# Perceiver block on one core: the row maxima go along the partitions by two DMAs through DRAM, and the second value product stands later in its slot

## The chip, the cores and the metric

The kernel runs on one core of a Trainium2 chip. The metric is device time in microseconds (us); smaller is better. The engines are named as in the profile: PE is TensorE's matrix product, PEld its weight load, DVE is VectorE, ACT ScalarE, POOL GpSimd and SP SyncE, which here only issues DMAs.

## The reference

A block of three parts on x (32 batches x 64 queries x 256), all in float32:

```python
# cross attention: 16 heads of 16 features, 1601 keys in each batch
qh = split_heads(layernorm(x) @ wq.T + bq)
kh = split_heads(ctx @ wk.T + bk)            # ctx: 32 x 1601 x 256
vh = split_heads(ctx @ wv.T + bv)
scores = where(mask, einsum('bhqd,bhkd->bhqk', qh, kh) / sqrt(16), -1e9)
x = x + merge(softmax(scores) @ vh) @ wo.T + bo

# span attention over the 64 queries: no keys, a weight by distance
span = heads(layernorm(x) @ W_span.T)        # two numbers for each query and head
mean, soft = sigmoid(span[..., 0]) * 64, softplus(span[..., 1])
x = x + merge(softmax(-soft * (pos - mean) ** 2) @ heads(h @ W_val.T)) @ W_out.T

# a shared gated unit and 2 of 8 experts, chosen by the token's number
x = x + ffn(layernorm(x))
```

What matters for the change is the softmax of the cross attention: from each score, the largest score of its query and head is taken off before the exponential.

## The kernel before, in words

**Tiles.** The work of the cross attention comes in 64 halves n = 0 to 63: batch b = n // 2 and, with c = n % 2, 8 of its 16 heads. The keys are padded to 13 chunks of 124. Scores stand with the keys along the partitions: `prob` keeps them as 124 partitions x (pair of heads j) x 13 chunks x 128, where 128 is two heads by 64 queries. A pair is 124 x 1664 numbers. A half has four pairs, j = 0 to 3. `prob` has five places of two pairs: pairs 0 and 1 of half n are in place n % 2, pairs 2 and 3 in place 2 + n % 3.

**Steps of a half.** TensorE projects keys (`pk`, L492, in four groups of 4, 3, 3 and 3 chunks, numbered 0 to 3) and values (`pv`, L492, in units of two chunks, numbered 0 to 6). ACT copies them out of PSUM into kT (L507) and v (L524). `scores(n, g)` with g = 0, 1, 2 computes 4, 5 and 4 chunks of scores (`psc`, L546), and DVE adds the mask while it moves them into `prob` (L570). The fifth chunk of g = 1 does not fit in the four PSUM banks of the others. It goes to one bank more and to `spare_pvs`, and DVE moves it with two adds of its own, which stand as A and B in the lists of order (L563). `spare_pvs` lies in the same PSUM tile as `pvs`, where the value products are summed. ACT copies the first chunk into `mrun` (L579), and DVE takes the running maximum over the 13 chunks (L587); the last one writes `mx`.

**The maxima.** `mx` still has 124 partial maxima, one in each partition. TensorE transposes it (`pm`, L594) and DVE reduces it along the row to `mc` (L601), 128 x 4: the maximum of each column of `prob`, with the column along the partitions. It is needed in every partition. So `maxima_along_rows` has TensorE transpose each column of `mc`, repeated 124 times, into a bank `pb` (L609), and ACT copies that to `mb` (L613), 128 x 4 x 128, one buffer. `less_maxima` (L618) takes it off a pair on POOL, in the last half on DVE. `exponentials` (L623) run on ACT, and `values` (L633) multiply the exponentials by the values into `pvs`; `values(n, r)` takes pairs 2r and 2r + 1.

**The order.** Inside `tc.manual_schedule` (L729) each of PE, DVE, ACT and POOL carries out its instructions in the order in which the program names them; SP is not in that list and is ordered by the scheduler. The loop at L766 has 63 slots, n = 0 to 62. Slot n finishes half n - 1, works on the maxima and the exponentials of half n, and computes the scores of half n + 1 and the projections of batch b + 1. A slot reads:

```python
values(n-1, 0); project_keys(0); steps(-1); exponentials(n-1, 3)
scores(n+1, 0, taken_off)         # with the transposes into pm, and mc between its adds
project_values(3) if c else project_keys(1)
m = maxima_along_rows(mc); less_maxima(n, 0)
run(3*n); values(n-1, 1)
scores(n+1, 1); exponentials(n, 0)
# c = 1: keys 1, values 4, keys 2     c = 0: keys 2, values 0, values 1
less_maxima(n, 1); steps(1); exponentials(n, 1); less_maxima(n, 2)
scores(n+1, 2); project_keys(3)
# c = 1: values 5, 6                  c = 0: values 2
less_maxima(n, 3); exponentials(n, 2)
```

Some projections are `tiled`: `product` (L483) then splits one into four that use 32 columns of TensorE's array each. `run` and `steps` carry on the generators `query_steps` (L449, the first layer norm and the queries of two batches) and `span_steps` (L239, the span attention of two batches). Its 23 steps are spread over STEPS (L232), in stretches of a third of a slot, so it comes round once in four slots. Two of its steps are spoken of later: POOL's product with the reciprocal total (L349) and PE's transposes of its result, `psa` (L357), one stretch later. The other PE steps are `po`, `po2`, `po3`, `pval`, `psp`, and `tr_q`, `pq`, `tr_h` and `tr_f` for queries and norms. POOL also carries out three small steps for each layer norm (L206 to L209).

**PSUM and loads.** All banks named here but `mrun` and `pvs` come from one pool of six, in turn; whoever takes a bank waits until its last reader is done. `piece_ahead` has SP load a piece of the context two batches ahead (`ct`, five buffers of 3 or 4 chunks each, 361 to 496 KB), `load_x` loads two batches of x (128 KB, five buffers). The feed-forward part follows at L905.

Of the kernel before, what the change touches and what calls it, by code (L numbers as in the profile page):

```python
# [15 lines left out]
F32 = mybir.dt.float32  # L16
U8 = mybir.dt.uint8
AF = mybir.ActivationFunctionType
ALU = mybir.AluOpType
AX = mybir.AxisListType  # L20
PSUM = bass.MemoryType.PSUM
IN_TURN = mybir.DependencyInfo(mybir.DependencyClass.Sync, mybir.DependencyReason.DATA)

P = 128
S = 64
D = 256
# [4 lines left out]
CHUNK = 124  # L31
NKC = 13
# [58 lines left out]
def perceiver_kernel(ctx: ExitStack, tc: tile.TileContext, a: dict[str, bass.AP], out: bass.AP):  # L91
    nc = tc.nc
# [7 lines left out]
    work = ctx.enter_context(tc.tile_pool(name="work", bufs=2))  # L100
# [21 lines left out]
    xs: dict[int, bass.AP] = {}  # L122
    kept = ctx.enter_context(tc.tile_pool(name="kept", bufs=1, space=bass.MemoryType.DRAM))
    x_kept = kept.tile([NTILE, P, D], F32, name="x_kept")

    def load_x(t: int):
        xs[t] = work.tile([P, D], F32, tag="x", bufs=5, name=f"x{t}")
        nc.sync.dma_start(out=xs[t], in_=a["x"][t * P : (t + 1) * P, :])

    def load_square(name: str, engine, width: int = D):  # L130
# [352 lines left out]
    def piece_ahead(b: int, g: int):  # L483
        if b < B:
            load_piece(b, g)
# [116 lines left out]
            col, ps[:, : 4 * CHUNK].rearrange("p (j k) -> p j k", j=4), AX.X, ALU.max  # L602
        )

    def maxima_along_rows(col):

        ps = mm_bank("pb")
        for j in range(4):
            nc.tensor.transpose(  # L609
                ps[:CHUNK, j * P : (j + 1) * P], col[:, j : j + 1].to_broadcast([P, CHUNK]), ident  # L610
            )
        m = work.tile([P, 4, P], F32, tag="mb", bufs=1, name="mb")
        nc.scalar.copy(m[:CHUNK].rearrange("p j q -> p (j q)"), ps[:CHUNK])  # L613
        return m

    def less_maxima(n: int, j: int, m, engine):
        sj = pair_of(n, j)
        engine.tensor_tensor(  # L618
            sj, sj, m[:CHUNK, j, None, :].to_broadcast([CHUNK, NKC, P]), ALU.subtract
        )  # L620

    def exponentials(n: int, j: int):
        nc.scalar.activation(pair_of(n, j), pair_of(n, j), AF.Exp)  # L623

    def values(n: int, r: int):

        b, c = halves[n]
        v = vs[b % 2]
        for k in range(NKC):
            kn = min(CHUNK, KEYS - k * CHUNK)  # L630
            for j in range(4):
                h = 4 * r + j
                nc.tensor.matmul(  # L633
                    pvs[32 * j : 32 * j + DK + 1, c, :, r, :],
                    lhsT=v[:kn, k, 8 * c + h, :],
                    rhs=pair_of(n, h // 2)[:kn, k, (h % 2) * S : (h % 2) * S + S],
                    start=(k == 0), stop=(k == NKC - 1), tile_position=(0, 32 * j),
                )
# [64 lines left out]
    def finish_steps(b: int, stretch: int):  # L703

        t = b // 2
        if b % 2 == 0:
            oT[t] = work.tile([P, 2, 2, S], F32, tag="oT", name=f"oT_{t}")
        flat = "p c u r q -> p (c u r q)"
        nc.vector.transpose(turned_pvs.rearrange(flat), pvs.rearrange(flat))
        by_head = turned_pvs.rearrange("p c u r i -> p (c u r) i")  # L710
        rec = work.tile([P, 8], F32, tag="rec", name=f"rec_{b}")
        nc.vector.reciprocal(rec, by_head[:, :, DK])
        o = work.tile([P, 8, DK], F32, tag="o", name=f"o_{b}")
        nc.vector.tensor_tensor(
            o, by_head[:, :, :DK], rec[:, :, None].to_broadcast([P, 8, DK]), ALU.mult
        )
        nc.vector.transpose(oT[t][:, :, b % 2, :], o.rearrange("p (c n) i -> p c (n i)", c=2))
        if b % 2:
            at = steps_of(t)
            agenda[stretch - 1 + at[0]].append((t, span_steps(t, oT.pop(t))))  # L720
            held_at.add(stretch - 1 + at[SMALL])
        yield
# [7 lines left out]
        tc.manual_schedule(  # L730
            engines={
                mybir.EngineType.PE, mybir.EngineType.DVE, mybir.EngineType.Activation,
                mybir.EngineType.Pool,
            }
        )
    )
# [25 lines left out]
        load_piece(1, g)  # L762
    last = len(halves) - 1

    extra = {3 * last - 3: (0,), 3 * last - 2: (1, 2, 4), 3 * last - 1: (5, 6)}
    for n, (b, c) in enumerate(halves[:-1]):  # L766
        if c == 0:
            piece_ahead(b + 2, 0)
            if b % 2 == 0 and b // 2 + 1 < NTILE:
                load_x(b // 2 + 1)  # L770
        if c and b % 2 == 0 and b // 2 + 1 < NTILE:
            agenda[3 * n].append((b // 2 + 1, query_steps(b // 2 + 1)))

        def project(f, *args):
            if b + 1 < B:
                f(b + 1, *args)

        def steps(g: int):
            run(3 * n + g)
            for u in extra.get(3 * n + g, ()):  # L780
                linear_factor(u)

        def taken_off():
            turned.extend(turned_maxima(n))
            return turned

        turned: list = []
        if n:
            values(n - 1, 0)
        project(project_keys, c, 0, True)  # L790
        if n:
            steps(-1)
            exponentials(n - 1, 3)
        if c:
            piece_ahead(b + 2, 1)
        scores(n + 1, 0, taken_off)
        if c:
            project(project_values, 3)
        else:
            project(project_keys, c, 1)  # L800
        m = maxima_along_rows(turned[1])
        less_maxima(n, 0, m, nc.gpsimd)
        held = 3 * n in held_at
        if not held:
            first_maxima(n + 1)
        run(3 * n)
        if n:
            values(n - 1, 1)
            if c == 0:
                agenda[3 * n + 1].append((b // 2, finish_steps(b - 1, 3 * n + 1)))  # L810
        for u in extra.get(3 * n, ()):
            linear_factor(u)
        if held:
            first_maxima(n + 1)
        else:
            for k in (1, 2) if c else (1, 2, 3):
                maximum(n + 1, k)

        scores(n + 1, 1, order=LATER if held else None if c else SOONER)
        exponentials(n, 0)  # L820
        if c:
            project(project_keys, c, 1)
            piece_ahead(b + 2, 2)
            project(project_values, 4)
            project(project_keys, c, 2)
            piece_ahead(b + 2, 3)
        else:
            project(project_keys, c, 2)
            for u in (0, 1):
                project(project_values, u)  # L830
        less_maxima(n, 1, m, nc.gpsimd)
        steps(1)
        exponentials(n, 1)

        less_maxima(n, 2, m, nc.gpsimd)
        scores(n + 1, 2)
        project(project_keys, c, 3, True)
        for u in (5, 6) if c else (2,):
            project(project_values, u, True)
        less_maxima(n, 3, m, nc.gpsimd)  # L840
        exponentials(n, 2)
# [5 lines left out]
    exponentials(last - 1, 3)  # L847
    turned = turned_maxima(last)
    maxima_of_rows(*turned)
    m = maxima_along_rows(turned[1])  # L850
    for j in range(4):
        less_maxima(last, j, m, nc.vector)
        exponentials(last, j)
# [165 lines left out]
```

## Time and profile before

| what | value |
|---|---|
| median of 3 runs | 1513.2 us (1512.55 to 1513.53) |
| the profiled execution | 1510.1 us, span 1508.3 us |
| granted TensorE clock, mean | 0.994 |
| PE busy | 1466.4 us (97%), 28600 products |
| DVE busy | 1226.2 us (81%) |
| POOL busy | 1120.2 us (74%) |
| ACT busy | 953.7 us (63%) |
| subtraction of the maxima on POOL (L618) | 252 of 3751 ns, 938.9 us |
| transposes into pb (L609) | 256, 40.4 us of PE |
| copy of pb to mb (L613) | 64 of 584 ns, 37.3 us of ACT |
| value products (L633) | 13312, 212.3 us of PE |

The span is the profiled execution's own length on the core; the time of the run has 1.8 us more around it. A row of the profile names the line in the code, the engine, the operation and the tiles as output<-input; then the number of instructions, their busy time and the mean of one, and the time that the engine was idle before them with what ended it. A chain is followed back from the last instruction: at each step to what released it, or to the instruction ahead of it on its engine.

### The profile page before, as it was taken

How to read it: one execution, taken by the hardware profiler on the slowest of the kernel's cores; microseconds unless marked ns; L12 is line 12 of the kernel's file. 1: busy time of each engine (PE TensorE's matmuls, PEld its weight loads, DVE VectorE, ACT ScalarE, POOL GpSimd, SP SyncE). 2: the span in 40 equal slices, each digit the busy share in tenths (PEclk: the TensorE clock that was granted, in tenths of full speed). 3: DMA queues.
4: the chain of work that ended last, by engine and by line, in shares of the span. 5: the costliest groups of instructions: out<-in, count | busy, mean ns of one | idle time of the engine just before them, and what ended most of it. 6: DMA issues, size and time to landing. Idle time of an engine off the chain costs nothing.

```text
span 1508.3 us, 62981 instructions
## 1 busy us (share of the span) xinstructions
PE 1466.4 (97%) x28600; PEld 1059.0 (70%) x28600; DVE 1226.2 (81%) x2332; ACT 953.7 (63%) x1727; POOL 1120.2 (74%) x508
## 2 busy tenths in 40 slices
PE   8999999999999999999999999999999999988899
PEld 5676777777676767777777767777777777654587
DVE  4889898998989898989989899989899898973100
ACT  3565667676776767586767767676767666766411
POOL 1677787988878887879888888878798888852710
PEclk9999999999999999999999999999999999999999
DMA  5211111111111111111111111111111111005100
GB/s 179 56 37 46 36 47 46 38 48 50 50 50 47 43 43 43 37 53 37 49 51 50 50 47 52 34 44 37 52 46 40 50 50 33 2 9 161 60 29 28
DMA packets 52220, 73.95 MB, mean 49 GB/s; under 512 B 3828, under 2 KB 51184, under 8 KB 51824
## 3 DMA queue, kind: packets, MB, share of 16 engines
q1 hardware_dynamic: 51136, 69.13, 16.1%
q8 instruction: 225, 3.69, 1.0%
q10 hardware_dynamic: 816, 0.79, 0.2%
q14 instruction: 43, 0.35, 0.1%
HBM read 65.71 MB, written 4.19 MB: 46 GB/s over the span
## 4 chain that ended last, share of the span: by engine, by line
PE 58%; DVE 20%; POOL 11%; ACT 8%; issue 2%; DMA 0%; ACTq 0%; DVEq 0%; POOLq 0%
PE pv L492 14%; PE pk L492 13%; POOL prob L618 9%; DVE prob L570 8%; PE pvs L633 7%; PE psc L546 7%; DVE mrun L587 7%; PE py L949 4%; PE u L662 2%; PE pb L609 2%; PE ph L931 2%; DVE mc L601 2%; ACT prob L623 2%; ACT qbd L474 1%; PE psa L357 1%
## 5 line engine op out<-in xcount | busy, mean ns | idle before, releaser
L618 POOL TENSOR_TENSOR prob<-prob,mb 124x1664 f32<-124x1664 f32 x252 | 938.9, 3751 | 217.2 <-ACT mb L613 160.4
L570 DVE TENSOR_TENSOR prob<-psc,madd 124x512 f32<-124x512 f32 x768 | 505.4, 682 | 76.1 <-PE psc L546 75.8
L623 ACT ACTIVATE prob<-prob 124x1664 f32<-124x1664 f32 x256 | 407.1, 1590 | 214.9 <-POOL prob L618 212.0
L587 DVE TENSOR_TENSOR mrun<-prob,mrun 124x512 f32<-124x512 f32 x704 | 486.6, 691 | 31.1 <-ACT mrun L579 17.3
L492 PE MATMUL pk<-ct,wkT_sb 128*32 128x496 f32 (+1 forms) x2512 | 398.9, 519 | 7.5 <-DMA wkT_sb<-in_wkT 5.4
L492 PE MATMUL pv<-wvT_sb,ct 128*124 128x256 f32 x3524 | 386.1, 379 | 0.6 <-DVE prob L563 0.5
L492 PEld LDWEIGHTS pv<-wvT_sb,ct 128*124 128x124 f32 x3524 | 270.3, 132 | 108.1 <-issue 19.4
L546 PEld LDWEIGHTS psc<-qbd,kT 32*124 32x124 f32 x6400 | 201.0, 181 | 63.5 <-issue 19.2
L546 PE MATMUL psc<-qbd,kT 32*124 32x128 f32 x6400 | 239.2, 279 | 2.7 <-issue 1.4
L492 PEld LDWEIGHTS pk<-ct,wkT_sb 128*32 128x32 f32 (+1 forms) x2512 | 146.6, 126 | 118.3 <-issue 59.0
L633 PEld LDWEIGHTS pvs<-prob,v 124*17 124x17 f32 x13312 | 197.3, 98 | 29.9 <-issue 16.2
L633 PE MATMUL pvs<-prob,v 124*17 124x64 f32 x13312 | 212.3, 220 | 1.6 <-ACT prob L623 1.6
L507 ACT ACTIVATE kT<-pk,cols 128x372 f32<-128x372 f32 (+2 forms) x256 | 150.0, 586 | 81.9 <-PE pk L492 81.7
L524 ACT COPY v<-pv 124x512 f32<-124x512 f32 (+1 forms) x224 | 124.1, 554 | 85.4 <-PE pv L492 84.0
L323 ACT ACTIVATE sc<-sc,least 128x64 f32<-128x64 f32 x256 | 85.6, 342 | 2.1 <-DVE least L319 2.1
L951 DVE SCALAR_TENSOR_TENSOR ot<-py,prob 128x256 f32<-128x256 f32 x16 | 6.8, 425 | 75.7 <-PE py L949 66.1
L662 PE MATMUL u<-xfT,sw_sb 128*128 128x512 f32 x128 | 60.9, 624 | 3.6 <-ACT prob L689 2.7
L579 ACT COPY mrun<-prob 124x512 f32<-124x512 f32 x64 | 38.0, 593 | 38.3 <-DVE soft L306 35.3
L546 PE MATMUL pvs<-qbd,kT 32*124 32x128 f32 x256 | 55.2, 294 | 0.2 <-issue 0.2
L323 ACT ACTIVATION_READ_ACCUMULATOR sc<-sc,least 128x1 f32 x256 | 50.0, 195 | 0.0
L609 PEld LDWEIGHTS pb<-cst,mc 128*124 128x124 f32 x256 | 28.8, 135 | 29.3 <-DVE mc L601 23.8
L938 ACT ACTIVATE hT<-ph,cols 128x256 f32<-128x256 f32 x32 | 13.4, 471 | 56.3 <-PE ph L931 56.3
(126 smaller groups left out, 1249.3 us busy)
## 6 DMA issues: line engine op xcount, KB each, us to landing
ct<-in_ctxT SPq DMA_DIRECT2D x64, 372.0 KB, 3.2
ct<-in_ctxT SPq DMA_DIRECT2D x32, 496.0 KB, 3.7
ct<-in_ctxT SPq DMA_DIRECT2D x32, 361.0 KB, 3.2
w<-in_w SPq DMA_DIRECT2D x16, 256.0 KB, 7.2
x<-in_x SPq DMA_DIRECT2D x17, 128.0 KB, 2.7
x_kept<-x SPq DMA_DIRECT2D x16, 128.0 KB, 1.7
prob<-x_kept SPq DMA_DIRECT2D x8, 256.0 KB, 6.2
out<-ot SPq DMA_DIRECT2D x16, 128.0 KB, 1.9
```

Of the source, the lines that this page charges most:

```text
L323: nc.scalar.activation(sc[:, h, :], sc[:, h, :], AF.Exp, bias=least[:, h : h + 1], scale=-1.0, accum_out=total[:, h : h + 1],)
L492: nc.tensor.matmul(out[at:end], lhsT=lhsT[:, at:end], rhs=rhs, start=start, stop=stop, **(dict(tile_position=(0, at)) if tiled else {}),)
L507: nc.scalar.activation(kTs[c][:, k0 : k0 + kn], ps[:, :kn], AF.Identity, bias=cols[:, B_K + c : B_K + c + 1])
L524: nc.scalar.copy(vs[b % 2][:kn, 2 * u : 2 * u + n, :, :DK], ps[:kn, : n * D].rearrange("p (n h d) -> p n h d", n=n, d=DK),)
L546: product = nc.tensor.matmul(ps[:CHUNK, at * P : (at + 1) * P], lhsT=kTs[c][32 * j : 32 * j + 32, k0 : k0 + CHUNK], rhs=qbd[b // 2][32 * j ...
L570: nc.vector.tensor_tensor(pair_of(n, j)[:, c0 : c0 + 4, :].rearrange("p k (e q) -> p k e q", e=2), pss[j][:CHUNK].rearrange("p (k e q) -> ...
L587: nc.vector.tensor_tensor(dst, block_of(n, k), run, ALU.max)
L618: engine.tensor_tensor(sj, sj, m[:CHUNK, j, None, :].to_broadcast([CHUNK, NKC, P]), ALU.subtract)
L623: nc.scalar.activation(pair_of(n, j), pair_of(n, j), AF.Exp)
L633: nc.tensor.matmul(pvs[32 * j : 32 * j + DK + 1, c, :, r, :], lhsT=v[:kn, k, 8 * c + h, :], rhs=pair_of(n, h // 2)[:kn, k, (h % 2) * S : ( ...
L662: nc.tensor.matmul(ps, lhsT=w[:, c, hc * P : (hc + 1) * P], rhs=xfT[:, c, :, slot], start=(c == 0), stop=(c == 1),)
L949: nc.tensor.matmul(py, lhsT=x, rhs=w, start=(n == 0), stop=(n == len(terms) - 1))
```

## The change

The first part replaces TensorE's and ACT's way to `mb` by DMAs in slots 0 to 62. `mc` (128 x 4) is written to a row of 512 numbers in DRAM, in pieces of four numbers (16 bytes) from each partition; two such rows, `m_kept`, are used in turn. A nop on SP waits for that transfer. Then one DMA reads the row into all 128 partitions: `mb`, 2 KB in each, 256 KB in all. In the row the four pairs j lie side by side for each column q, so `mb` is now 128 x 128 x 4, and `less_maxima` reads the numbers of a pair in steps of four, 16 bytes. `mb` has two buffers. The last half keeps the transposes (`last_maxima_along_rows`); its copy writes in steps of four numbers.

The second part is the order in a slot. SP is now in the manual order as well, so its DMAs are issued as the program names them. `less_maxima(n, 1)` stands right after `less_maxima(n, 0)`, ahead of `run(3 * n)`. `exponentials(n - 1, 3)` stands after `scores(n + 1, 1)`. `values(n - 1, 1)` moves from ahead of `scores(n + 1, 1)` to behind it and two groups of keys. With c = 0 the third group of keys (number 3) comes earlier and whole, and value units 0 and 1 are tiled and stand on the two sides of `scores(n + 1, 2)`; with c = 1 value unit 4 is tiled and follows both groups of keys. x has six buffers instead of five, and the early units of the feed-forward part (`extra`) are spread otherwise.

```diff
--- before.py
+++ after.py
@@ -122,9 +122,10 @@
     xs: dict[int, bass.AP] = {}
     kept = ctx.enter_context(tc.tile_pool(name="kept", bufs=1, space=bass.MemoryType.DRAM))
     x_kept = kept.tile([NTILE, P, D], F32, name="x_kept")
+    m_kept = [kept.tile([4 * P], F32, name=f"m_kept{i}") for i in range(2)]
 
     def load_x(t: int):
-        xs[t] = work.tile([P, D], F32, tag="x", bufs=5, name=f"x{t}")
+        xs[t] = work.tile([P, D], F32, tag="x", bufs=6, name=f"x{t}")
         nc.sync.dma_start(out=xs[t], in_=a["x"][t * P : (t + 1) * P, :])
 
     def load_square(name: str, engine, width: int = D):
@@ -602,21 +603,32 @@
             col, ps[:, : 4 * CHUNK].rearrange("p (j k) -> p j k", j=4), AX.X, ALU.max
         )
 
-    def maxima_along_rows(col):
+    def maxima_along_rows(n: int, col):
+
+        row = m_kept[n % 2]
+        down = nc.sync.dma_start(out=row.rearrange("(q j) -> q j", j=4), in_=col)
+        tc.add_manual_dep(nc.sync.nop().ins, down.ins.name, IN_TURN, reason="row")
+        m = work.tile([P, P, 4], F32, tag="mb", bufs=2, name="mb")
+        nc.sync.dma_start(out=m.rearrange("p q j -> p (q j)"), in_=row.partition_broadcast(P))
+        return m
+
+    def last_maxima_along_rows(col):
 
         ps = mm_bank("pb")
         for j in range(4):
             nc.tensor.transpose(
                 ps[:CHUNK, j * P : (j + 1) * P], col[:, j : j + 1].to_broadcast([P, CHUNK]), ident
             )
-        m = work.tile([P, 4, P], F32, tag="mb", bufs=1, name="mb")
-        nc.scalar.copy(m[:CHUNK].rearrange("p j q -> p (j q)"), ps[:CHUNK])
+        m = work.tile([P, P, 4], F32, tag="mb", bufs=2, name="mb")
+        nc.scalar.copy(
+            m[:CHUNK].rearrange("p q j -> p j q"), ps[:CHUNK].rearrange("p (j q) -> p j q", j=4)
+        )
         return m
 
     def less_maxima(n: int, j: int, m, engine):
         sj = pair_of(n, j)
         engine.tensor_tensor(
-            sj, sj, m[:CHUNK, j, None, :].to_broadcast([CHUNK, NKC, P]), ALU.subtract
+            sj, sj, m[:CHUNK, None, :, j].to_broadcast([CHUNK, NKC, P]), ALU.subtract
         )
 
     def exponentials(n: int, j: int):
@@ -730,7 +742,7 @@
         tc.manual_schedule(
             engines={
                 mybir.EngineType.PE, mybir.EngineType.DVE, mybir.EngineType.Activation,
-                mybir.EngineType.Pool,
+                mybir.EngineType.Pool, mybir.EngineType.SP,
             }
         )
     )
@@ -762,7 +774,7 @@
         load_piece(1, g)
     last = len(halves) - 1
 
-    extra = {3 * last - 3: (0,), 3 * last - 2: (1, 2, 4), 3 * last - 1: (5, 6)}
+    extra = {3 * last - 2: (0, 1, 2), 3 * last - 1: (4, 5, 6)}
     for n, (b, c) in enumerate(halves[:-1]):
         if c == 0:
             piece_ahead(b + 2, 0)
@@ -790,24 +802,22 @@
         project(project_keys, c, 0, True)
         if n:
             steps(-1)
-            exponentials(n - 1, 3)
         if c:
             piece_ahead(b + 2, 1)
         scores(n + 1, 0, taken_off)
+        m = maxima_along_rows(n, turned[1])
         if c:
             project(project_values, 3)
         else:
             project(project_keys, c, 1)
-        m = maxima_along_rows(turned[1])
         less_maxima(n, 0, m, nc.gpsimd)
+        less_maxima(n, 1, m, nc.gpsimd)
         held = 3 * n in held_at
         if not held:
             first_maxima(n + 1)
         run(3 * n)
-        if n:
-            values(n - 1, 1)
-            if c == 0:
-                agenda[3 * n + 1].append((b // 2, finish_steps(b - 1, 3 * n + 1)))
+        if n and c == 0:
+            agenda[3 * n + 1].append((b // 2, finish_steps(b - 1, 3 * n + 1)))
         for u in extra.get(3 * n, ()):
             linear_factor(u)
         if held:
@@ -817,24 +827,30 @@
                 maximum(n + 1, k)
 
         scores(n + 1, 1, order=LATER if held else None if c else SOONER)
-        exponentials(n, 0)
+        if n:
+            exponentials(n - 1, 3)
         if c:
             project(project_keys, c, 1)
             piece_ahead(b + 2, 2)
-            project(project_values, 4)
             project(project_keys, c, 2)
-            piece_ahead(b + 2, 3)
         else:
             project(project_keys, c, 2)
-            for u in (0, 1):
-                project(project_values, u)
-        less_maxima(n, 1, m, nc.gpsimd)
+            project(project_keys, c, 3)
+        exponentials(n, 0)
+        if n:
+            values(n - 1, 1)
+        project(project_values, 4 if c else 0, True)
+        if c:
+            piece_ahead(b + 2, 3)
         steps(1)
-        exponentials(n, 1)
 
         less_maxima(n, 2, m, nc.gpsimd)
         scores(n + 1, 2)
-        project(project_keys, c, 3, True)
+        if c:
+            project(project_keys, c, 3, True)
+        else:
+            project(project_values, 1, True)
+        exponentials(n, 1)
         for u in (5, 6) if c else (2,):
             project(project_values, u, True)
         less_maxima(n, 3, m, nc.gpsimd)
@@ -847,7 +863,7 @@
     exponentials(last - 1, 3)
     turned = turned_maxima(last)
     maxima_of_rows(*turned)
-    m = maxima_along_rows(turned[1])
+    m = last_maxima_along_rows(turned[1])
     for j in range(4):
         less_maxima(last, j, m, nc.vector)
         exponentials(last, j)
```

## The prediction

> **What bounds the kernel now.** I read the busy shares first, then the chain that ended last, then the groups of L609 and L618 with their waits, then two slots of the timeline. The page, engines and chain:
>
> ```profile
> PE 1466.4 (97%) x28600; PEld 1059.0 (70%) x28600; DVE 1226.2 (81%) x2332; ACT 953.7 (63%) x1727; POOL 1120.2 (74%) x508
> ...
> PE 58%; DVE 20%; POOL 11%; ACT 8%; issue 2%; DMA 0%; ACTq 0%; DVEq 0%; POOLq 0%
> ```
>
> TensorE (PE) is busy nearly throughout. But 39% of the chain runs over VectorE (DVE), GpSimd (POOL) and ScalarE (ACT): they are just in time, with little slack. The windows view over two periods of four slots (duration, then busy time of PE, PEld, DVE, ACT, POOL):
>
> ```profile
> 1026.10:1108.65 82.55, 81.81 (x1766) 59.56 (x1766) 74.78 (x143) 56.91 (x105) 68.82 (x30) 1.00 0.17 46
> 1108.65:1191.12 82.47, 81.73 (x1767) 59.48 (x1766) 74.78 (x143) 56.92 (x105) 68.90 (x30) 1.00 0.17 46
> ```
>
> A period repeats to 0.1 us, so one period tells what 62 slots do. POOL works 68.9 of 82.5 us. I call the first value product of a slot S. In the timeline S stands at 1083.67, 1104.90, 1124.15, 1144.55 and again 1166.14, so slots last 21.23 (kind A, n = 3 mod 4), 19.25 (B, 0), 20.40 (C, 1) and 21.59 us (D, 2). Rows of a kind A slot (start, duration):
>
> ```profile
> 1083.67 1.64 PE L633 MATMUL pvs<-prob,v 124*17 124x64 f32 x104
> ...
> 1090.15 0.67 DVE L601 TENSOR_REDUCE mc<-pm 128x4 f32<-128x496 f32 x1
> ...
> 1091.07 0.60 PE L609 MATMUL pb<-cst,mc 128*124 128x128 f32 x4
> ...
> 1092.42 3.71 POOL L618 TENSOR_TENSOR prob<-prob,mb 124x1664 f32<-124x1664 f32 x1 [4.74 <-ACT mb L613]
> ...
> 1094.98 0.42 DVE L563 TENSOR_TENSOR prob<-psc,madd_fifth 124x256 f32<-124x256 f32 x1
> ...
> 1096.05 1.89 PE L492 MATMUL pv<-wvT_sb,ct 128*124 128x256 f32 x8
> 1096.10 1.90 POOL L349 TENSOR_TENSOR sc<-sc,total 128x1024 f32<-128x1024 f32 x1
> ...
> 1097.70 0.42 DVE L563 TENSOR_TENSOR prob<-pvs,madd_fifth 124x256 f32<-124x256 f32 x1
> ...
> 1099.02 1.04 PE L357 MATMUL psa<-cst,sc 128*128 128x128 f32 x8
> ```
>
> The maxima are ready (mc) at S+7.15, and POOL subtracts them 1.6 us later. DVE's two fifth-block adds, "add A" and "add B", end at S+11.75 and S+14.45; PE comes past add A with something to do. The waits view (us in total, times, longest):
>
> ```profile
> POOL prob L618 <- ACT mb L613: 160.4, 47, 11.5
> PEld pb L609 <- DVE mc L601: 23.8, 31, 1.0
> DVE prob L563 <- PE pvs L546: 3.7, 6, 2.1
> ```
>
> POOL does wait for mb; but DVE's fifth-block adds almost never wait for PE. A faster PE won't bring them forward.
>
> **Removed.** Per slot the transposes into pb (0.44 us of PE, 0.60 where they wait) and the ACT copy (37.3 us over 64, 584 ns each, not on the path). PE: 63 x 0.44 = 28 us, and of the waits for mc 7 us (the PE row) to 24 us (its weight load's row) more. That is all that can be won. Projections that change between tiled and whole differ by at most 0.13 us a unit, up in some and down in others: nothing.
>
> **Added: a route with two transfers.** Neither occurs before. Row to DRAM: 2 KB in 128 pieces; the nearest row is the 128 KB store of x_kept, 1.7 us. Back, repeated over 128 partitions, 256 KB: between x (128 KB, 2.7) and ct (361 or 372 KB, 3.2), so 2.9. With 0.2 for SP's waiting, 1.7 + 2.9 + 0.2 = 4.8 us from mc to POOL's start, where the trace has 1.6. Bounds: 1.7 + 2.7 = 4.4; and 8.3, if one ct load (3.2) stands ahead in the queue and the broadcast takes 3.2. I take 4.8, since SP's loads are spread over the slot. mb is then ready at S+12.0 (A), 11.7 (B), 11.2 (C, D). What queues behind the wait on SP: pieces 2 and 3 of ct and the x loads. They are needed a slot later and land in about 3 us: nothing, unless SP were held for a whole slot. The store of x_kept is read only in the tail: nothing.
>
> **Changed: the subtraction's second operand** now steps 16 bytes from element to element. No POOL row of before does that. The nearest is L618 itself (3751 ns for 1664 elements, both operands contiguous); that is the low end, and I exclude less. From POOL's rows with two contiguous operands (L893 256 elements 724 ns, L898 512 in 1264, L618) an element costs 2.14 ns; L349, whose second operand is one number repeated along a row (1024 in 1903 ns), gives 1.67. Reading a second stream thus costs 0.47 ns an element, 0.78 us an instruction. Estimates: that share doubled gives 4.5 us, fourfold (one useful element of each 16 bytes) 6.1. I take 4.5, the nearest to the row that isn't free, and keep 3.75 and 6.1 for the range.
>
> [...]
>
> **Moved.** (1) less(n,1) goes ahead of the span steps, so POOL L349 (kind A) stands behind two subtractions. PE's transposes psa (L357) wait for it, and PE works in order. (2) values(n-1,1), 1.46 us, leaves its place ahead of the second scores, where it covered DVE, and now stands behind add B, since add B reads the PSUM tile that it writes. (3) In c=0 pk3, in c=1 pk2 now come as the projection that needs the PSUM bank of add A. DVE's order isn't changed, so A and B still end where they do; PE arrives at them 1.46 + 0.44 us earlier and idles. Slot 0, which has no values yet, shows this wait in before:
>
> ```profile
> 48.54 0.42 DVE L563 TENSOR_TENSOR prob<-psc,madd_fifth 124x256 f32<-124x256 f32 x1
> ...
> 49.01 1.34 PE L492 MATMUL pv<-wvT_sb,ct 128*124 128x256 f32 x5 [0.54 <-DVE prob L563]
> ```
>
> **The sum**, with p for one subtraction, and PE's pieces from the chain of waits: values 1.46, pk3 1.35 (pk2 1.25), a tiled pv unit 1.73, pv5 and 6 2.59, scores 1.08, psa 0.87.
> - A (13 slots with psa): mb 12.0 + 2p + L349 1.9 + psa 0.87 + scores 1.08 + pk3 1.35 + pv5,6 2.59 + 0.2 = 27.5 at p = 3.75, 29.0 at 4.5. Change +6.2, +7.8. Two slots of that kind without psa: 14.4 (add B) + 1.46 + 1.73 + 1.08 + 1.35 + 2.59 + pval 1.06 = 23.7, +2.5.
> - B (15): add A 11.2, then pk3, add B 12.7, values, pv0, po2 0.45, scores, pv1, pv2: 12.7 + 1.46 + 1.73 + 0.45 + 1.08 + 3.46 + 0.45 for two short ACT waits = 21.35; at 4.5 the next slot's first values come later still, as they need exp(n,1): 11.7 + 9.0 + 1.6 + 0.1 = 22.4. Change +2.1, +3.15.
> - C (16): add B 14.6 + 1.46 + 1.73 + 1.08 + 1.35 + 2.59 + 0.35 = 23.15; at 4.5 the third subtraction of slot B ends 11.7 + 13.5 - 22.4 = 2.8 us into this one; its exponential (1.6) and the key copy behind it on ACT (0.67) hold the first scores to 5.1 instead of 3.9, so 24.35. Change +2.75, +3.95.
> - D (16): add B 12.65, values, pv0, po3 0.87, pq 0.91, psp 0.25, two tr 0.44, scores, pv1, pv2 = 22.9, with 0.1 of waits 23.0; at 4.5 the same lateness, with POOL's six small statistics steps (2.5 us), adds 0.8: 23.8. Change +1.4, +2.25.
>
> At p = 3.75: 13 x 6.2 + 5 + 15 x 2.1 + 16 x 2.75 + 16 x 1.4 = 184. At p = 4.5: 13 x 7.8 + 5 + 15 x 3.15 + 16 x 3.95 + 16 x 2.25 = 253. By the same steps, p = 5.2 gives 329 and 6.1 gives 422. The 28 us removed are inside these sums: they show as PE's earlier arrival. Each us of the route beyond 4.8 adds about 44 (A, B and D wait on it). The profiled run is 1510.1 (span 1508.3); the median of the runs is 3 higher. So 1510 + 3 + 253 = 1766, **1765**.
>
> **Rivals.**
> - The strided read is free (p = 3.75): 1513 + 184 = 1697. For it: POOL at 2.2 ns an element may not be limited by reading. Against: the second stream costs 0.47 ns of them. Chance 0.29 (1660 to 1730).
> - It is dear (p of 5.2 to 6.1, or a route of 6 us or more): 1842 to 1935. POOL would then work 68.9 + 16 x 1.45 = 92 us of each period or more and nearly be the bound. Chance 0.22, 0.08 of it above 1890.
> - DVE follows the earlier PE: if adds A and B came 1.5 us earlier in each slot, 1697 - 62 x 1.5 = 1604. Against it the 3.7 us of L563's waits for PE. Chance 0.07 (1530 to 1640).
> - Other side: PE stays the bound, its holes are filled, and the transposes are saved: 1513 - 28 to 1513 - 52, about 1480. It decides only if add A ends by the time PE comes to it, some 2 us earlier than the rows show, and L349 ends by S+15 instead of S+21. Chance 0.03.
> - No change to measure: 0.01. The main case, p about 4.5 (1730 to 1810): 0.38.
>
> A change under 0.2% (3 us) can't be told from none here. Slower: 0.38 + 0.29 + 0.22 + 0.07 = 0.96; faster 0.03; same 0.01. Left out of 1640 to 1890 are 0.07 + 0.04 + 0.08, so the range holds 0.81.
>
> **What would show it.** [...] It is wrong if PE stays above 93% busy, if the adds move with PE, or if the route takes 6 us or more.

## The result and the profile after

The changed kernel takes **1874.9 us** (median of 4 runs, 1872.2 to 1877.8) against 1513.0 (1512.6 to 1513.5) for the kernel before, a ratio of 1.239, with a 95% interval of 1.237 to 1.242. The forecast was 1765, with a range of 1640 to 1890: the sign and the range held, but the size fell short, 252 us forecast and 362 measured. The profiled execution took 1872.8 us, its span is 1871.0.

The page of the profile after, engines and the group of the subtraction (busy time, mean of one, idle time before and what ended most of it):

```profile
PE 1554.4 (83%) x30208; PEld 1039.8 (56%) x30208; DVE 1238.9 (66%) x2332; ACT 918.9 (49%) x1664; POOL 1344.8 (72%) x508
...
L630 POOL TENSOR_TENSOR prob<-prob,mb 124x1664 f32<-124x1664 f32 x252 | 1164.4, 4652 | 347.9 <-DMA mb<-m_kept 213.3
```

The subtraction went from 3751 to 4652 ns. No engine is the bound any more: PE stands still 17% of the time, and it is busy for longer than before (1554 against 1466 us) though the transposes are gone. The clock, below, explains a part of that (its mean is 0.959, before it was 0.994); how much of the rest comes with its 30208 products, 28600 before, wasn't measured apart. The chain of the page can't be used here: its shares cover 14% of the span.

The DMA view after, with bytes and the median time to landing:

```profile
mb<-m_kept SPq DMA_DIRECT2D x63, 256.0 KB, 4.1
...
m_kept<-mc SPq DMA_DIRECT2D x63, 2.0 KB, 1.4
```

The waits view after:

```profile
PE psa L358 <- POOL sc L350: 91.5, 16, 7.1
...
PE pvs L645 <- ACT prob L635: 55.7, 43, 7.0
...
PE pk L493 <- DVE prob L564: 46.9, 57, 1.3
...
PE pvs L645 <- DVE prob L564: 30.5, 32, 3.3
...
DVE prob L564 <- PE pvs L547: 0.2, 1, 0.2
```

Three waits of PE, 6 us or less each before, are large now: for POOL's product (psa, 92 us), for VectorE's two fifth-block adds (47 + 31) and for exponentials (56). Waits for ScalarE's copies of keys and values add some 61 us. The adds themselves wait for PE 0.2 us in all, and in the slot below they end at S+12.55 and S+15.27, where before it was S+11.75 and S+14.45: they did not follow PE.

The kind A slot of the timeline after that begins at 1042.80 and ends at 1075.49; the last row is from slot C, two slots on:

```profile
1049.93 0.67 DVE L602 TENSOR_REDUCE mc<-pm 128x4 f32<-128x496 f32 x1
1050.63 0.32 SPq L609 DMA_DIRECT2D m_kept<-mc  x1
1053.29 0.32 SPq L612 DMA_DIRECT2D mb<-m_kept  x1
...
1055.40 1.52 PE L493 MATMUL pk<-ct,wkT_sb 128*128 128x372 f32 x4 [0.40 <-DVE prob L564]
1056.61 9.14 POOL L630 TENSOR_TENSOR prob<-prob,mb 124x1664 f32<-124x1664 f32 x2 [4.60 <-DMA mb<-m_kept]
...
1058.13 1.65 PE L645 MATMUL pvs<-prob,v 124*17 124x64 f32 x104 [1.21 <-DVE prob L564]
...
1065.71 1.90 POOL L350 TENSOR_TENSOR sc<-sc,total 128x1024 f32<-128x1024 f32 x1
...
1067.66 1.97 PE L358 MATMUL psa<-cst,sc 128*128 128x128 f32 x8 [6.16 <-POOL sc L350]
...
1069.55 2.08 PE L547 MATMUL psc<-qbd,kT 32*124 32x128 f32 x32
...
1071.57 1.51 PE L493 MATMUL pk<-ct,wkT_sb 128*32 128x361 f32 x16
...
1099.43 1.58 PE L645 MATMUL pvs<-prob,v 124*17 124x64 f32 x98 [2.12 <-ACT prob L635]
```

The maxima are ready at 1050.60, POOL starts at 1056.61: 6.0 us where before it was 1.6. In the four slots of one period (D, A, B, C) the route takes 5.90, 6.01, 6.19 and 5.83 us; the median of all 63 is 6.0. PE waits for add A, then for add B, then 6.16 us for the product. Slots D, A, B, C of this period last 23.60, 32.69, 21.53 and 26.62 us, 104.4 together; over the twelve periods between the first and the thirteenth of these products the mean is 106.1 (before 82.7).

One thing more is in those rows: the eight transposes take 1.97 us where the same ones took 1.04 before, and the scores behind them 2.08 instead of 1.15. The windows around them (PE, PEld, DVE, ACT, POOL busy, then granted clock, DMA share, GB/s):

```profile
1061.00:1066.00 5.00, 0.50 (x12) 0.02 (x3) 0.89 (x2) 2.07 (x2) 5.00 (x3) 0.90 0.27 74
1066.00:1068.00 2.00, 0.34 (x2) 0.34 (x3) 0.00 (x0) 0.00 (x0) 2.00 (x2) 0.50 0.00 0
1068.00:1070.00 2.00, 2.00 (x16) 1.67 (x18) 0.00 (x0) 0.93 (x2) 2.00 (x1) 0.50 0.00 0
1070.00:1072.00 2.00, 2.00 (x39) 1.54 (x39) 0.34 (x1) 0.25 (x1) 2.00 (x1) 0.55 0.00 0
```

PE has nothing to do from 1061.5; from about 1065.0 (a mean of 0.90 over 5 us is 1 us at half) the granted clock is half, and it comes back near 1071.8, some 4 us after the work began again. This wait of 6.16 us so cost about 2 us more than itself (1.97 and 2.08 us instead of 1.04 and 1.15).

### The profile page after: what moved, and what is told of

It reads as the page before. It is cut to its first block, busy times and chain, and to the rows that moved or that the text cites. A ratio compares the mean times of both kernels' runs of the same rounds, so it can differ in the third digit from the quotient of the medians.

```text
span 1871.0 us, 66438 instructions
## 1 busy us (share of the span) xinstructions
PE 1554.4 (83%) x30208; PEld 1039.8 (56%) x30208; DVE 1238.9 (66%) x2332; ACT 918.9 (49%) x1664; POOL 1344.8 (72%) x508
## 5 line engine op out<-in xcount | busy, mean ns | idle before, releaser
L630 POOL TENSOR_TENSOR prob<-prob,mb 124x1664 f32<-124x1664 f32 x252 | 1164.4, 4652 | 347.9 <-DMA mb<-m_kept 213.3
L493 PE MATMUL pk<-ct,wkT_sb 128*32 128x496 f32 (+1 forms) x2140 | 418.2, 550 | 84.5 <-DVE prob L564 46.9
L493 PE MATMUL pv<-wvT_sb,ct 128*32 128x256 f32 (+1 forms) x5756 | 398.1, 382 | 32.4 <-ACT kT L508 19.0
L493 PEld LDWEIGHTS pv<-wvT_sb,ct 128*32 128x32 f32 (+1 forms) x5756 | 216.1, 113 | 171.2 <-ACT v L525 23.4
L645 PE MATMUL pvs<-prob,v 124*17 124x64 f32 x13312 | 231.7, 224 | 87.5 <-ACT prob L635 55.7
L493 PEld LDWEIGHTS pk<-ct,wkT_sb 128*32 128x32 f32 (+1 forms) x2140 | 165.2, 138 | 225.2 <-DVE prob L564 82.8
L645 PEld LDWEIGHTS pvs<-prob,v 124*17 124x17 f32 x13312 | 207.6, 100 | 145.6 <-DVE prob L564 67.6
L547 PE MATMUL psc<-qbd,kT 32*124 32x128 f32 x6400 | 274.2, 292 | 7.3 <-issue 1.0
L547 PEld LDWEIGHTS psc<-qbd,kT 32*124 32x124 f32 x6400 | 226.4, 190 | 91.8 <-issue 54.8
L358 PE MATMUL psa<-cst,sc 128*128 128x128 f32 x128 | 31.3, 426 | 91.5 <-POOL sc L350 91.5
L358 PEld LDWEIGHTS psa<-cst,sc 128*128 128x128 f32 x128 | 24.9, 222 | 99.1 <-POOL sc L350 99.1
L360 ACT COPY aT<-psa 128x512 f32<-128x512 f32 x32 | 18.8, 587 | 82.6 <-PE psa L358 82.6
```

What stands on the lines that cost most here:

```text
L358: nc.tensor.transpose(ps[:, i * P : (i + 1) * P], scf[:, n * P : (n + 1) * P], ident)
L493: nc.tensor.matmul(out[at:end], lhsT=lhsT[:, at:end], rhs=rhs, start=start, stop=stop, **(dict(tile_position=(0, at)) if tiled else {}),)
L547: product = nc.tensor.matmul(ps[:CHUNK, at * P : (at + 1) * P], lhsT=kTs[c][32 * j : 32 * j + 32, k0 : k0 + CHUNK], rhs=qbd[b // 2][32 * j ...
L630: engine.tensor_tensor(sj, sj, m[:CHUNK, None, :, j].to_broadcast([CHUNK, NKC, P]), ALU.subtract)
L645: nc.tensor.matmul(pvs[32 * j : 32 * j + DK + 1, c, :, r, :], lhsT=v[:kn, k, 8 * c + h, :], rhs=pair_of(n, h // 2)[:kn, k, (h % 2) * S : ( ...
```

## The experiments

The theory after the result: three causes share the loss, the longer route (6.0 instead of 1.6 us), the dearer read (0.9 us, four times a slot) and the order, with the half clock behind the wait of 6.16 us on top. The rivals make one of the three the cause and the others harmless. I took the three apart, alone and in pairs. Times are to be held against 1513 and 1875; runs of before beside them gave 1510 to 1512.

**The read, side by side.** The edit in the changed kernel:

```diff
-            sj, sj, m[:CHUNK, None, :, j].to_broadcast([CHUNK, NKC, P]), ALU.subtract
+            sj, sj, m.rearrange("p q j -> p (q j)")[:CHUNK, None, j * P : (j + 1) * P]
+                .to_broadcast([CHUNK, NKC, P]), ALU.subtract
```

> The changed kernel, with the subtraction reading 128 numbers side by side from the broadcast row instead of every fourth. It so takes off the maxima of other columns; one number still goes for all keys of a column, which a softmax doesn't notice. Route and order stay. Theory (three causes that share the loss: a route of some 6 us instead of 1.6, a read that costs 0.9 us more, and the new order): the subtraction falls from 4650 to 3750 ns; kind A slots lose two of these, 1.8 us, the others 0.4 to 0.9, in all about 50 us, so 1795 to 1840. Rival, the strided read is the cause: below 1600. Rival, the read is hidden: 1870 to 1880.

Measured: 1767.7, below the range of 1795 to 1840, with the subtraction at 3746 ns. The stride costs 107 us here, twice what the theory had, but far from all: neither the read alone nor a hidden read.

**The second subtraction back.**

```diff
         less_maxima(n, 0, m, nc.gpsimd)
-        less_maxima(n, 1, m, nc.gpsimd)
...
             piece_ahead(b + 2, 3)
+        less_maxima(n, 1, m, nc.gpsimd)
         steps(1)
```

> The changed kernel with the second subtraction back behind the projections, so that POOL's product with the reciprocal total (L350) runs ahead of it. Theory: the wait of 6 to 7 us of TensorE's transposes for that product, once in four slots, goes (13 x some 5 to 7 us, with the half clock after it), but the exponential of the second pair and with it the next slot's first values come 1.9 us later in two slots of four: 1800 to 1850. Rival, this order is most of the loss: below 1700. Rival, the wait only moves to the values: 1865 or more.

Measured: 1846.3. In one slot (1047.16 of its timeline) the transposes now wait 1.82 us and take 1.09 us, and the scores behind them 1.15, as before; their waits sum to 28 us instead of 92. But PE's waits for exponentials at the values rise from 56 to 80 us, and the mean granted clock is no better (0.953 against 0.959). So this order costs 29 us, and more than half of its wait moves on.

**The values back.** `values(n - 1, 1)` ahead of the second scores and `exponentials(n - 1, 3)` ahead of the first, as before:

```diff
             steps(-1)
+            exponentials(n - 1, 3)
...
         run(3 * n)
+        if n:
+            values(n - 1, 1)
...
-        if n:
-            exponentials(n - 1, 3)
...
-        if n:
-            values(n - 1, 1)
```

> The changed kernel with the second value product and the fourth exponential back in their old places. Theory: in the changed kernel the fourth subtraction of the slot before runs up to 12 us into the slot, so that the values, in the old place, wait for its exponential until 9 to 13 us into the slot, and the second scores behind them: 1835 to 1915, no clear gain. Rival, the move of the values is a main cause, as it leaves TensorE waiting for VectorE's fifth-chunk adds (1 to 2 us a slot): 1790 or less.

Measured: 1900.6. With maxima this late, the old place is no better, but worse: PE waits for the product 8.80 us in one slot (1083.05 of its timeline).

**Route and read without the moves.** The kernel before, with `maxima_along_rows` and `less_maxima` of the changed kernel and SP in the manual order (and its sixth buffer of x):

```diff
         scores(n + 1, 0, taken_off)
+        m = maxima_along_rows(n, turned[1])
...
-        m = maxima_along_rows(turned[1])
         less_maxima(n, 0, m, nc.gpsimd)
```

> The kernel before with the two DMAs and the strided read, and none of the moves but SyncE's order. By the theory: POOL's four subtractions end 13 + 4 x 4.65 + 2.2 for other work = 33.8 us after the slot's start; the second values of the next slot need the exponential behind them (1.6), and some 12.5 us of TensorE's work follow them, so a slot lasts (33.8 + 1.6 + 12.5) / 2 = 24 instead of 20.6 us: about 1725, 1690 to 1800. So the new order would cost some 100 us beside the route. Rival, the order was made for the route and helps it: 1880 or more. Rival, the route is harmless in this order: below 1560.

Measured: 1878.3, and my number was far off: it lies 2 us below the rival that had the order made for the route. Without any of the moves the loss is as large as with all of them. What my sum left out is seen better in the run with the route alone, below.

**The order without the route.** The changed order with the old `maxima_along_rows` and its side-by-side `mb`:

```diff
-        nc.sync.dma_start(out=m.rearrange("p q j -> p (q j)"), in_=row.partition_broadcast(P))
+        ps = mm_bank("pb")
+        for j in range(4):
+            nc.tensor.transpose(
+                ps[:CHUNK, j * P : (j + 1) * P], col[:, j : j + 1].to_broadcast([P, CHUNK]), ident
+            )
+        m = work.tile([P, 4, P], F32, tag="mb", bufs=2, name="mb")
+        nc.scalar.copy(m[:CHUNK].rearrange("p j q -> p (j q)"), ps[:CHUNK])
```

> The changed kernel's order with the old route: transposes, copy, a contiguous read (3750 ns). Theory: TensorE still comes too early to VectorE's fifth-chunk adds, and the product that the transposes of kind A wait for stands behind two subtractions, but 3 us earlier: +2.8 (A), +2.1, +2.75, +1.4 us a slot, about 140 in all, 1600 to 1690. Rival, the order is harmless with fast maxima: 1500 to 1530. Rival, the order is most of the loss: 1750 or more.

Measured: 1705.3, above the theory's range. But the run isn't clean: the transposes stood directly behind the first scores, where the changed kernel has its DMA, and PE waited for the maxima there (79.4 us in 53 waits), ten times as long as in the kernel before (7.2). So I ran it again with the transposes behind the projection:

```diff
-        m = maxima_along_rows(n, turned[1])
         if c:
             project(project_values, 3)
         else:
             project(project_keys, c, 1)
+        m = maxima_along_rows(n, turned[1])
```

> The run with the changed order and the old route put the transposes of the maxima ahead of the projection, where TensorE waited 1.5 us for them in 53 slots, which no other kernel here does. Here they stand behind the projection as in the kernel before, so that only the moves are new. Theory: those 79 us go, 1605 to 1650, and 90 to 140 us are left for the order itself. Rival, TensorE then waits as long for VectorE's adds: 1690 to 1710. Rival, the order costs nothing: 1500 to 1530.

Measured: 1643.1, within the range. The order alone costs 130 us. Rows of its timeline, with the two waits for the fifth-block adds that the prediction counted on:

```profile
1061.62 1.52 PE L493 MATMUL pk<-ct,wkT_sb 128*128 128x372 f32 x4 [1.27 <-DVE prob L564]
1063.75 1.65 PE L634 MATMUL pvs<-prob,v 124*17 124x64 f32 x104 [0.61 <-DVE prob L564]
```

**The read alone.** The kernel before; its copy spreads the maxima in steps of four numbers, POOL reads them so:

```diff
-        m = work.tile([P, 4, P], F32, tag="mb", bufs=1, name="mb")
-        nc.scalar.copy(m[:CHUNK].rearrange("p j q -> p (j q)"), ps[:CHUNK])
+        m = work.tile([P, P, 4], F32, tag="mb", bufs=1, name="mb")
+        nc.scalar.copy(
+            m[:CHUNK].rearrange("p q j -> p j q"), ps[:CHUNK].rearrange("p (j q) -> p j q", j=4)
+        )
```

> The kernel before, with its transposes, in which ScalarE's copy spreads the maxima in steps of four numbers and POOL reads them so. Only the stride is new. Theory: the subtraction takes 4650 ns, POOL then has 83 us of work for each period of 82.5, and the values wait for it: a slot of (8.75 + 4 x 4.65 + 2.2 + 0.5 + 1.6 + 12.5) / 2 = 22.1 instead of 20.6 us, 1560 to 1650. Rival, the read is hidden: 1510 to 1530. Rival, it is most of the loss: 1750 or more.

Measured: 1688.1 (+175), above the range. The groups by form of this run, subtraction and copy:

```profile
L620 POOL TENSOR_TENSOR prob<-prob,mb 124x1664 f32<-124x1664 f32 x252 | 1160.8, 4639 | 172.0 <-ACT mb L613 150.8 <-DVE mrun L304 21.2
...
L613 ACT COPY mb<-pb 124x512 f32<-124x512 f32 x64 | 72.1, 1126 | 1.9 <-PE pb L609 1.7
```

The copy, which writes in steps of 16 bytes here, takes 1126 instead of 584 ns; that is about 0.5 us of the delay, so this run prices the copy along with the read. PE's waits in it are 65 us for exponentials at the values and 51 us for key copies.

**The row written twice.**

```diff
         tc.add_manual_dep(nc.sync.nop().ins, down.ins.name, IN_TURN, reason="row")
+        down = nc.sync.dma_start(out=row.rearrange("(q j) -> q j", j=4), in_=col)
+        tc.add_manual_dep(nc.sync.nop().ins, down.ins.name, IN_TURN, reason="row")
```

> The changed kernel with the row written twice, each time waited for, ahead of the broadcast: the route becomes 1.5 to 2.3 us longer. Theory (every microsecond of the route costs about 44 in all): 1935 to 1985. Rival, the route is hidden behind other waits: 1870 to 1885.

Measured: 1985.4 (+110). In four slots the route lasts 7.66, 7.31, 8.31 and 8.99 us, 2.1 longer than in the changed kernel, so a microsecond of it costs about 53 (a single run, at the upper end of the theory). No wait hides it.

**A busy wait.** 40 transposes of the identity ahead of the ones that wait, once in four slots:

```diff
+FILL = 40
...
             ps = mm_bank(f"psa_{t}_{q}")
+            for k in range(FILL if q == 0 else 0):
+                nc.tensor.transpose(ps[:, k % 4 * P : (k % 4 + 1) * P], ident, ident)
```

> The changed kernel with 40 transposes of the identity on TensorE ahead of the ones that wait for POOL's product, into the same bank, which is overwritten. In the changed kernel the granted clock is 0.50 for some 5 us after that wait, and the 8 transposes take 1.97 instead of 1.04 us, the scores behind them 2.08 instead of 1.15. Theory: a wait that is filled keeps the clock at 1.0 and saves 1.9 us in 16 slots: 1835 to 1860. Rival, the slow stretch isn't on the path, or the clock doesn't depend on the wait: 1870 to 1880. Rival, the added work costs time itself: above 1880.

Measured: 1829.5 (1827.2 to 1837.4), a ratio to before of 1.212 (1.209 to 1.216), which doesn't touch the changed kernel's 1.237 to 1.242. **More work on PE made the kernel 45 us faster**, more than the theory's 15 to 40: the transposes and scores account for some 30 us (1.9 in 16 slots), and where the other 15 come from isn't shown. The timeline and the windows of this run at the same step:

```profile
1038.53 4.59 PE L358 MATMUL psa<-cst 128*128 128x128 f32 x40
1044.59 1.09 PE L361 MATMUL psa<-cst,sc 128*128 128x128 f32 x8 [1.47 <-POOL sc L351]
```

```profile
1046.00:1048.00 2.00, 2.00 (x48) 1.18 (x48) 1.22 (x3) 0.35 (x1) 2.00 (x1) 1.00 0.00 0
```

POOL's product comes as late as ever, but the clock stays at 1.00 and the transposes take 1.09 us.

**The route alone**: the run with route and read, with the side-by-side read of the first experiment.

> The kernel before's order with the two DMAs, and a subtraction that reads side by side (so it takes off the maxima of other columns, one number for all keys of a column still): the route alone, without the stride and without the moves. The run with route and stride took 1878, that with the stride alone 1688, so the route cost 190 there, 3 us a slot for a route that is 4.6 us longer. Theory (a late subtraction costs through ScalarE's queue and the values, once the slack is used up): the route alone uses the slack first and costs 110 to 190, 1620 to 1705. Rival, route and stride add up: 1695 to 1710. Rival, the route alone is hidden: below 1560.

Measured: 1812.3 (+299), well above the theory and all its rivals: the route is the largest of the three by itself. Its timeline shows what my sums for the old order had left out:

```profile
939.01 3.71 POOL L630 TENSOR_TENSOR prob<-prob,mb 124x1664 f32<-124x1664 f32 x1 [8.94 <-DMA mb<-m_kept]
...
942.75 1.59 ACT L635 ACTIVATE prob<-prob 124x1664 f32<-124x1664 f32 x1 [4.56 <-POOL prob L630]
944.25 0.55 ACT L508 ACTIVATE kT<-pk,cols 128x372 f32<-128x372 f32 x1
...
944.95 1.32 PE L358 MATMUL psa<-cst,sc 128*128 128x128 f32 x8 [3.74 <-ACT kT L508]
...
946.20 2.08 PE L547 MATMUL psc<-qbd,kT 32*124 32x128 f32 x32
```

The exponential stands ahead of the key copies in ScalarE's queue. It waits for POOL, the copies wait behind it, and PE waits for the copies, 3.74 us here; then the scores take 2.08 us, as they did at half the clock, instead of 1.15. The mean granted clock of this run is 0.927. PE's waits for key copies in this run, with 22.2 us more at `psp`:

```profile
PE psc L547 <- ACT kT L508: 105.6, 34, 4.1
PE psa L358 <- ACT kT L508: 50.9, 13, 4.3
```

**One move alone.** To test that, one of the moves of the changed kernel, the first exponential behind the projections, in the run with the route alone:

```diff
-        exponentials(n, 0)
         if c:
             project(project_keys, c, 1)
...
             for u in (0, 1):
                 project(project_values, u)
+        exponentials(n, 0)
```

> The run with the route alone (the order of before, a read side by side, 1812), with one move of the changed kernel: the first exponential stands behind the projections that follow the second scores. In that run ScalarE stands 4.6 to 7.8 us in each slot at this exponential, which waits for POOL, and the key copies behind it hold TensorE for 3 to 4 us, with a half clock after most of these waits. Theory: this queue is what the late subtraction costs; with the copies ahead of it the next bound is the first values of the next slot, which need two exponentials, 13 + 7.5 + 1.6 = 22.1 us after the slot's start, 24 where POOL's span work stands between: 1640 to 1735. Rival, the second values hold the slot as well and take the gain back: 1780 to 1815. Rival, the copies aren't what holds TensorE: no change, 1805 to 1820 or more.

Measured: 1742.0 (1739.8 and 1744.1): 70 us less than with the old place, and 7 us above the upper end of the theory. The waits for key copies fall from 179 to 27 us. The values' wait for exponentials, which the theory named, is now the largest, and psa's wait for POOL's product, which it did not name, comes next:

```profile
PE pvs L645 <- ACT prob L635: 102.9, 59, 5.2
PE psa L358 <- POOL sc L350: 56.6, 16, 5.5
```

**A try at a faster kernel.** Since the route lost in every form, I went back to the kernel before and tried to take away PE's wait for the maxima:

```diff
-    "0 1 t 2 3",
+    "0 t 1 2 3",
```

> The kernel before, in which VectorE reduces the maxima after one of the four adds instead of two. TensorE's transposes wait for the maxima in about half of the slots there (7 us by its products, 24 us by its weight loads). Theory: the maxima come 0.68 us sooner, those waits go, and the subtraction starts sooner: 1490 to 1508. Rival, the second add then holds something else by as much: 1510 to 1520. Rival, VectorE waits for the transposes into the bank: above 1520.

Measured: 1523.5 (1519.4 to 1525.6), ratio 1.008 (1.005 to 1.010): 0.8% slower, where the theory had it faster. PE's wait for the maxima fell from 7.2 to 0.8 us, but PE's product `po` now waits 15 us for key copies, which it didn't, and VectorE waits for the transposes of the maxima 4.0 us in 17 slots (0.8 in one before), as the last rival had it. That accounts for the sign, not for every microsecond. No kernel of this study beats the one before.

The three parts together:

| order | read | route | us | against before |
|---|---|---|---|---|
| old | side by side | transposes | 1513 | |
| new | side by side | transposes | 1643 | +130 |
| old | stride | transposes | 1688 | +175 |
| old | side by side | DMAs | 1812 | +299 |
| new | side by side | DMAs | 1768 | +255 |
| old | stride | DMAs | 1878 | +365 |
| new | stride | DMAs (the change) | 1875 | +362 |

Alone the parts cost 604 us, together 362. They are paid on the same path (maxima, subtraction, exponential, values), so they share what one of them has already opened. The order costs 130 where the maxima are early, saves 44 (1812 to 1768) where they are late, and with the stride too makes no difference (1878, 1875). The eighth combination wasn't run, and SP's manual order was never run by itself: it comes with every row but the first and the third. PE's and PEld's waits for pieces of the context are some 2 us at most in the runs with it, 1.2 before. Most rows are single runs, and four runs of the busy wait differ by 10 us, so differences of that size among them mean nothing.

## Why the prediction fell short though its range held

- **The subtraction** was priced at 4.5 us from the slope of POOL's rows (the second stream's share doubled); it took 4.65. Right. The whole instruction rose by 24%, from 3751 to 4652 ns.
- **The route** is the step that failed: "1.7 + 2.9 + 0.2 = 4.8 us". It took 5.8 to 6.2, 6.0 at the median. The mis-sized term is the broadcast: its landing was 4.1 us at the median, not 2.9 (the estimate came from plain loads of x and ct). The row to DRAM landed in 1.4, sooner than the 1.7 that it was given, though between the issues of the two transfers lay 1.5 to 2.7 us. The prediction's own sign of being wrong, a route of 6 us or more, holds for about half of the 63 halves. The price of a microsecond, 44, was somewhat low: the doubled row gives 53. So 1.2 us more made about 53 to 64 us.
- **A term was missing: the clock.** The sum put psa at 0.87 and scores at 1.08 us behind a wait of several microseconds. After the wait of 6.16 us they took 1.97 and 2.08, at a granted clock of 0.50. The busy wait puts the price of this one place at 45 us. The mean granted clock is 0.959, and in the busy wait's run, with this wait filled, still 0.983 (before: 0.994): clock is lost at other places too, and their part wasn't measured apart.
- **Slot by slot**, the rows shown bear this out. The kind A slot lasts 32.69 us where the sum had 29.0: its maxima come 0.65 later (at S+7.80), the route takes 1.2 more, and psa and the scores take 3.91 together (1067.66 to 1071.57) instead of 1.95. In slot B the next values wait for the second exponential until 1099.43, 23.94 us after the slot's start, where the sum had 22.4; that is the route again. (Four products of slot C run ahead of this wait, at 1097.02, so slot B counts as 21.53.) By the changes that the sum has for the four kinds, a period was to last 95 (p = 3.75) to 100 us (p = 4.5), and it lasts 106.
- **psa behind POOL's product**: the sum for A has PE done with add B, the values and a value unit at S+17.6, and the product at S+21.4 to S+22.9, so a wait of 3.8 to 5.3 us once in four slots; measured 5.7 in the mean of 16, 7.1 at most. Right in place and nearly in size. Undoing it was worth only 29 us, while the values' wait for exponentials grew by 24.
- **PE at add A and add B**: forecast, and seen in 62 slots by its weight loads (82.8 and 67.6 us), in 57 and 32 by its products; the adds didn't move with PE. The order alone, 130 us, tests this step without the route and the read. With p = 3.75 and a route of 4.8 us the prediction had 184; the run with the new order, the DMAs and the side-by-side read took 255: again the route and the clock, as far as the rows above show.
- **The 28 us removed** were said to show only as an earlier arrival of PE. No kernel here tests that alone, and every one with the DMAs is slower than before.
- Adding the corrections to the 253 gives 253 + 53 (route, at 44) + 16 (0.15 us of the subtraction at 108, from the prediction's 253 and 329) + 45 (clock) = 367, against 362. That it closes so well is partly luck, since the table shows that such terms don't add.
- **The rivals**: dear read or long route, given 0.22 (1842 to 1935), is where the time fell, by the route (and the clock, which no rival had) and not by the read. The free read is refuted by 4652 ns, "DVE follows" by add A and B, which come later and not sooner, the faster outcome by all of these.

What stays open: how much of the 299 us of the route alone is the queue and how much the clock; the move of one exponential gave 70 back, and the waits for key copies sum to 179. I also didn't take ScalarE's other exponentials out of the way.

## What to carry to other kernels

Before giving an engine's work to a DMA because the engine is the bound, follow what hangs on the result: here 0.44 us of PE a slot was traded for 4.4 us on a path with little slack, and the in-order queues (ScalarE's exponential ahead of the key copies, POOL's subtraction ahead of the span product) passed the delay to PE several times over. Price a small transfer by its whole way, issue to first use, two landings (1.4 and 4.1 us here) and what lies between them, 6.0 us in all; and where a bound engine is to wait several microseconds, look at its granted clock afterwards too: here a wait of 6.16 us cost about 2 us beyond itself. Try parts of a change in pairs as well as alone: the order that costs 130 us with early maxima gives 44 back with late ones.

## What the runs showed of the hardware

- **In TensorE's waits of 6 us ahead of psa the granted clock fell to half.** In the slot shown it fell to 0.50 some 3.5 us into the wait of 6.16 us; in the twelve waits of 6.02 to 7.10 us ahead of psa it fell 3.0 to 5.4 us into them, and it read 0.50 until 3.4 to 6.2 us after the work began again. These runs show no sharp threshold. The same eight transposes took 1.09 us after a wait of 1.82 us (the second subtraction back), 1.32 after 3.74 (the route alone), and 1.97 after 6.16 (the changed kernel) and 8.80 (the values back); in between it goes either way, 1.97 after a wait of 3.61 us in the changed kernel (at 1669.83 of its timeline) and 1.09 after one of 3.58 in the run with one move alone (at 1088.02).
- **The reads and the write in steps of 16 bytes were dearer on three engines**: POOL's subtraction 3751 to 4652 ns (+24%), VectorE's in the last half 1886 to 3240 (+72%), and ScalarE's copy that writes so 584 to 1126 (+93%). VectorE's and ScalarE's rows, from the groups by form of the changed kernel and of the read alone, stand for 4 and 64 instructions.
- **Writing 128 pieces of 16 bytes to DRAM** landed in 1.4 us at the median, not longer than a 128 KB store (2.0 in the same run); the 256 KB broadcast, 4.1 us, is what made the route long.
